# A two-layer transformer on one core: the order of results in the gated unit's groups

## The chip, the cores and the metric

One Trainium2 chip, one core of it. The metric is device time of one execution in microseconds. The kernel before took 1144.48 us, the median of 3 runs (1144.44 to 1144.59). Differences of a few tenths of a per cent matter here.

## The reference

Four sequences of 512 tokens with 256 features pass through two layers in fp32; each half layer normalises its input and adds its result to the residual. Layer 0 is causal attention with 16 heads and a mixture of 8 experts; layer 1 is attention with 16 query and 4 key heads, and a gated unit with weights of 4 bits. Only the last matters here:

```python
def _L1_ffn_ref(x, gate_W_packed, gate_scales, ...):
    ...
    Wg = dequant_nvfp4(gate_W_packed, gate_scales)
    ...
    gate = jnp.einsum('th,nh->tn', xt, Wg)
    up = jnp.einsum('th,nh->tn', xt, Wu)
    gelu = jnp.tanh(0.7978845608028654 * (gate + 0.044715 * gate ** 3)) * gate * 0.5 + gate * 0.5
    inter = gelu * up
    out = jnp.einsum('tn,hn->th', inter, Wd)
```

It has 2048 tokens, 256 features and 2048 inner units.

## The kernel before

**Engines and order.** TensorE (PE), VectorE (DVE), ScalarE (ACT) and GpSimd (POOL) run their instructions in the order in which the program writes them. The program is therefore a schedule written by hand: where a call stands decides where its instruction stands in its engine's queue. Only semaphores between engines make one wait for another.

**The last stage.** The gated unit runs over 4 blocks of 512 tokens (`j`) and, in each, 8 groups of 256 inner units (`jj`): 32 groups, `i = 8 j + jj`, in the loop at L1471. Groups 0 to 3 multiply plainly. Groups 4 to 31 (L1517 on, the branch that is changed) use a 2 x 2 scheme with 7 products in place of 8. Each `quarter` is one product: two matmuls, one for the gate weights and one for the up weights, which the trace shows as 4 matmul instructions. Besides the plain quarters of weights (`a11`, `a12`, `a22`) and tokens (`b11` and so on) the products read three sums of weights `s1`, `s2`, `s4`, the difference `s3` that takes the place of `a21`, and four sums of tokens `t`.

The products go into four PSUM tiles of 512 columns: `e` and `g`, two halves of `eg` (two buffers in turn), and `f` and `k` (one buffer each, called `gu_first` in the profile). The order on TensorE in one group is e, k, two down products, f, e, two down products, g, f, two down products, g, one down product. Between them stand:
- the copy f<-e (L1523), the copy p7<-k (L1529) and the copy g<-f (L1535) on ScalarE: the products after it add to what was copied;
- two additions on VectorE, `sb` upper = p7 + g (L1541) and `sb` lower = p7 + f (L1543). L1541 reads g before the last product adds to it, so that product waits for L1541.

**The results of the group before.** A group's gate and up values lie in `eg` (first half of the tokens) and `sb` (second half). Two generators make the activation of the *preceding* group, `eg_gelu` and `sb_gelu`, in four steps each: Square on ScalarE (L1405); a product on VectorE (L1407); Tanh on ScalarE (L1409); two products on VectorE, `th` and `it` (L1411, L1412). `done(i - 1)` then has GpSimd make three differences of the result `it` (L1314 with 512 columns, L1315 and L1316 with 256).

**Down products.** `down(n)` issues n matmuls of the second matrix product (L1336), which lags by two to three groups. Seven products take two groups. Their results go through ScalarE copies (L1348, L1356), VectorE additions (L1350, L1352, L1354, L1358, L1360) and, every second group, four GpSimd additions (L1362 to L1365). The two PSUM tiles `yx` and `yy` are used again by the next round: its first product needs L1360 of the round before to have read `yx`.

**Beside them.** `both()`, called twice in a group, advances the preparation of the next block: in group `jj` = 2 statistics (L1439, L1440), in 4 the normalising (four L1448), in 5 two transposes (L209) with DMAs issued by SP, in 7 the four token sums `t[0]`, `t[2]`, `t[1]`, `t[3]` (L1196 to L1199). `weight_sums(m)` makes s1, s3, s2, s4 of group `m` of every block (L1183, L1184, L1187, L1188), four additions on VectorE; for `jj` = 0 to 3 they are made in groups 4 to 7 and first read in groups 8 to 11.

Of the kernel before, what the change touches and what calls it, by code (L numbers as in the profile page):

```python
# [32 lines left out]
def tile_transformer(  # L33
# [18 lines left out]
    nc = tc.nc  # L52
# [411 lines left out]
    with ExitStack() as l0:  # L464
# [407 lines left out]
        done = blanked = 0  # L872
# [78 lines left out]
    def quarter(ps, terms, start=True):  # L951

        for i, (lhs, rhs) in enumerate(terms):
            for w in range(2):
                nc.tensor.matmul(  # L955
                    ps[:, w], lhsT=lhs(w), rhs=rhs, start=start and not i and not w,
                    stop=i == len(terms) - 1 and w == 1, skip_group_check=not start,
                )

    def unit(half, jj, par):  # L960
        return lambda w: wgu[:, w, half, jj, par * P : (par + 1) * P]

    def tokens(xT, half, n):
        return xT[:, half, n * 256 : (n + 1) * 256]

    def plainly(ps, xT, jj, par, n):
        quarter(ps, [(unit(half, jj, par), tokens(xT, half, n)) for half in range(2)])

    with ExitStack() as l1:
# [204 lines left out]
        def weight_sums(jj):  # L1174

            tt = nc.vector.tensor_tensor
            a11, a12, a21, a22 = (
                wgu[:, :, half, jj, par * P : (par + 1) * P] for par in range(2) for half in range(2)
            )
            s1, s2, s4 = (sums[jj - 4][:, :, i] for i in range(3))  # L1180

            def first():
                tt(s1, a21, a22, ALU.add)  # L1183
                tt(a21, a11, a21, ALU.subtract)  # L1184

            def second():
                tt(s2, s1, a11, ALU.subtract)  # L1187
                tt(s4, a12, s2, ALU.subtract)  # L1188

            return first, second  # L1190
# [89 lines left out]
    with ExitStack() as f1:  # L1280
# [16 lines left out]
        def down_unit(k, jj, m):  # L1297
            return wd[:, jj, k, m * P : (m + 1) * P]

        def down_weight_sums(jjs):  # L1300

            pool_tt = nc.gpsimd.tensor_tensor
            a11, a12, a21, a22 = (down_unit(k, jjs, m) for m in range(2) for k in range(2))
            s1, s2, s4 = (down_sums[:, jjs, i] for i in range(3))
            pool_tt(s1, a21, a22, ALU.add)
            pool_tt(a21, a11, a21, ALU.subtract)
            pool_tt(s2, s1, a11, ALU.subtract)
            pool_tt(s4, a12, s2, ALU.subtract)

        def unit_sums(i):  # L1310

            it = its[i]
            pool_tt = nc.gpsimd.tensor_tensor
            pool_tt(it[:, 4:6], it[:, 1:4:2], it[:, 0:2], ALU.subtract)  # L1314
            pool_tt(it[:, 6], it[:, 3], it[:, 4], ALU.subtract)  # L1315
            pool_tt(it[:, 1], it[:, 2], it[:, 6], ALU.subtract)  # L1316
# [55 lines left out]
        def down(n):  # L1372
            nonlocal next_down
            for _ in range(n):
                if next_down is not None and i >= 2 * next_down + 3:
                    next_down = next(downs, None)
# [49 lines left out]
        def done(i):  # L1426

            if i < NBLK * NJ - 2:
                unit_sums(i)
# [37 lines left out]
        f, k = firsts  # L1467
# [3 lines left out]
        for i in range(NBLK * NJ):  # L1471
            j, jj = divmod(i, NJ)
            if i == 3:
                nc.scalar.copy(last_a21, down_unit(0, slice(6, 8), 1))
            if i < 4:
                down_weight_sums(slice(2 * i, 2 * i + 2))
            if jj == 2 and j + 1 < NBLK:
                coming = next_inputs(j + 1)
            its[i] = d5.tile([P, 7, 256], F32, tag="it", name=f"it{i}")
            xT = xTs_f[j]  # L1480
            b11, b12, b21, b22 = (tokens(xT, half, n) for half in range(2) for n in range(2))
            if i < 2:
                egs.append(ps_eg.tile([P, 2, 2, 256], F32, tag="eg", name=f"eg{i}"))
            eg = egs[i % 2]
            e, g = eg[:, 0], eg[:, 1]
            sb = d2.tile([P, 2, 512], F32, tag="sb", name=f"sb{i}")
            eg_gelu, sb_gelu = before

            def both():
                if coming is not None:  # L1490
                    next(coming, None)

            if i < 4:
                eg_gelu.step()
                if not i:
                    nc.vector.tensor_copy(sb[:, :, :256], f)
                    nc.vector.tensor_copy(sb[:, :, 256:], k)
                plainly(e, xT, jj, 0, 0)
                sb_gelu.step()
                eg_gelu.step()  # L1500
                plainly(g, xT, jj, 0, 1)
                sb_gelu.step()
                eg_gelu.step()
                eg_gelu.step()
                sb_gelu.step()
                down(4)
                if i:
                    plainly(f, xT, jj, 1, 0)
                    nc.vector.tensor_copy(sb[:, :, :256], f)
                    sb_gelu.step()  # L1510
                    done(i - 1)
                    both()
                    down(3)
                    plainly(k, xT, jj, 1, 1)
                    nc.vector.tensor_copy(sb[:, :, 256:], k)
                    both()
            else:  # L1517
                t = [ts_f[j][:, n] for n in range(4)]
                s1, s2, s4 = (lambda w, n=n: sums[jj - 4][:, w, n] for n in range(3))
                a11, a12, s3, a22 = (unit(half, jj, par) for par in range(2) for half in range(2))  # L1520
                p7 = d2.tile([P, 2, 256], F32, tag="p7", name=f"p7_{i}")
                quarter(e, [(a11, b11)])
                nc.scalar.copy(f, e)  # L1523
                eg_gelu.step()
                eg_gelu.step()
                quarter(k, [(s3, t[2])])
                down(2)
                quarter(f, [(s2, t[1])], start=False)
                nc.scalar.copy(p7, k)  # L1529
                sb_gelu.step()  # L1530
                sb_gelu.step()
                eg_gelu.step()
                eg_gelu.step()
                quarter(e, [(a12, b21)], start=False)
                nc.scalar.copy(g, f)  # L1535
                sb_gelu.step()
                down(2)
                quarter(g, [(s1, t[0])], start=False)
                sb_gelu.step()
                done(i - 1)  # L1540
                tt(sb[:, :, 256:], p7, g, ALU.add)  # L1541
                quarter(f, [(a22, t[3])], start=False)
                tt(sb[:, :, :256], p7, f, ALU.add)  # L1543
                down(2)
                both()
                quarter(g, [(s4, b22)], start=False)
                down(1)
                both()
                if 4 <= i < 8:
                    for half in weight_sums(i - 4):  # L1550
                        half()
            before = (
                Gelu(f"{i}_0", eg[:, :, 0], eg[:, :, 1], its[i][:, 0:2]),
                Gelu(f"{i}_1", sb[:, 0], sb[:, 1], its[i][:, 2:4].rearrange("p n q -> p (n q)")),
            )
        eg_gelu, sb_gelu = before
# [76 lines left out]
```

## Time and profile before

| what | value |
|---|---|
| median of the runs | 1144.48 us |
| the profiled execution, its time and its span | 1144.61 us, 1142.9 us |
| granted TensorE clock | 1.00 throughout |
| 858 to 897 us (groups 4 to 7): TensorE, VectorE, GpSimd busy | 36.35, 35.55, 18.19 of 39 |
| 897 to 936 us (groups 8 to 11) | 37.90, 30.06, 16.87 of 39 |
| 936 to 1128 us (groups 12 to 31) | 187.62, 138.44, 83.96 of 192 |

A timeline row has the start and the busy time in microseconds, the engine, the line, the operation, the tile written and the tiles read, and the number of instructions that it merges; in brackets the idle time ahead of it and what ended it. Successive instructions of one engine overlap a little, so a row can start before the one ahead of it has ended. PEld is the weight load of a matmul, which can run beside the matmul before it.

### The profile page before, as it was taken

To read this page: it belongs to the slowest core of one execution; us is meant where nothing else is said; L and a number is where in the kernel's file an instruction comes from. 1 tells how busy PE (TensorE), PEld (TensorE's weight loads), DVE (VectorE), ACT (ScalarE), POOL (GpSimd) and SP (SyncE) were. 2 spreads that over 40 slices of the span, in tenths; PEclk is the share of its full clock that TensorE was granted. 3 is DMA by queue.
4 is the path that set the end of the run, shared out by engine and by line. 5 is a ranking of instruction groups with operands and counts; after the bars stand their busy time and mean duration, and the time that the engine had idled before them with its cause. 6 is when DMAs were issued, how large, how long until landed. Compare 5 with 4: busy or idle time off the path is not lost.

```text
span 1142.9 us, 19523 instructions
## 1 busy us (share of the span) xinstructions
PE 1113.0 (97%) x7474; PEld 716.1 (63%) x7474; DVE 844.6 (74%) x1856; ACT 509.8 (45%) x1190; POOL 247.1 (22%) x319
## 2 busy tenths in 40 slices
PE   9999999999999999999999999999999999999998
PEld 5666555555555445555555556656787788888885
DVE  6676989999988962867772695577479877778665
ACT  1445545565555543444444353344324444444442
POOL 8322221211112000000000000000064544353433
PEclk9999999999999999999999999999999999999999
DMA  4450110000000400000000001242001002002000
GB/s 133 113 130 2 21 20 1 2 1 2 1 2 1 156 29 1 1 1 1 1 1 0 1 1 38 65 111 65 20 1 45 30 19 74 1 19 74 18 3 19
DMA packets 30510, 34.92 MB, mean 31 GB/s; under 512 B 4280, under 2 KB 21432, under 8 KB 30416
## 3 DMA queue, kind: packets, MB, share of 16 engines
q1 hardware_dynamic: 29600, 32.49, 10.4%
q10 hardware_dynamic: 816, 1.18, 0.4%
q8 instruction: 59, 0.97, 0.3%
q14 instruction: 35, 0.29, 0.1%
HBM read 23.17 MB, written 6.29 MB: 26 GB/s over the span
## 4 chain that ended last, share of the span: by engine, by line
PE 69%; DVE 22%; ACT 3%; issue 2%; POOL 1%; SPq 1%; DMA 1%; DVEq 0%; POOLq 0%; ACTq 0%
PE qk_ps L1029 10%; PE lg_ps L249 9%; PE o L1120 8%; PE eo L249 7%; PE eg L955 7%; PE gu_first L955 5%; PE s L731 3%; PE yx L1336 3%; DVE mx L702 3%; PE s L683 3%; PE av L767 2%; PE yy L1336 2%; DVE it L1412 2%; DVE th L1411 2%; PE qk_ps L554 2%
## 5 line engine op out<-in xcount | busy, mean ns | idle before, releaser
L1029 PE MATMUL qk_ps<-xT,wqkv 128*128 128x512 f32 x320 | 148.7, 599 | 3.5 <-ACT v L1015 1.7
L249 PE MATMUL lg_ps<-rw,xT 128*128 128x512 f32 x256 | 122.5, 601 | 1.4 <-ACT xT L996 0.3
L249 PE MATMUL eo<-ew,xT 128*128 128x512 f32 x256 | 121.5, 600 | 0.8 <-ACT lg L312 0.5
L1120 PE MATMUL o<-wpj,oT 128*128 128x256 f32 x512 | 119.1, 382 | 0.0
L750 POOL TENSOR_SCALAR_AFFINE_SELECT pt<-pt 128x256 f32<-128x256 f32 (+2 forms) x88 | 62.4, 716 | 246.6 <-ACT pt L740 246.5
L1120 PEld LDWEIGHTS o<-wpj,oT 128*128 128x128 f32 x512 | 96.0, 190 | 27.0 <-issue 13.5
L1029 PEld LDWEIGHTS qk_ps<-xT,wqkv 128*128 128x128 f32 x320 | 59.1, 190 | 73.2 <-issue 58.4
L702 DVE TENSOR_REDUCE mx<-s 128x1 f32<-128x384 f32 (+3 forms) x176 | 100.4, 632 | 0.0
L740 ACT ACTIVATE pt<-s 128x512 f32<-128x512 f32 (+1 forms) x176 | 84.1, 564 | 35.8 <-PE s L731 35.8
L182 POOL TENSOR_TENSOR ln_rs<-rs_v,minus_half 128x4 f32<-128x4 f32 x12 | 13.6, 1131 | 366.2 <-DVE rs_v L181 366.2
L338 ACT ACTIVATE part<-eo,c 128x256 f32<-128x256 f32 x128 | 53.6, 472 | 84.6 <-PE eo L249 74.7
L1523 ACT COPY gu_first<-eg 128x512 f32<-128x512 f32 x28 | 16.0, 570 | 134.2 <-PE eg L955 129.9
L249 PEld LDWEIGHTS lg_ps<-rw,xT 128*128 128x128 f32 x256 | 46.1, 190 | 46.1 <-issue 37.3
L249 PEld LDWEIGHTS eo<-ew,xT 128*128 128x128 f32 x256 | 46.1, 190 | 45.7 <-issue 38.3
L312 ACT COPY lg<-lg_ps 128x512 f32<-128x512 f32 x64 | 37.7, 588 | 73.5 <-PE lg_ps L249 73.5
L1314 POOL TENSOR_TENSOR it<-it 128x512 f32<-128x512 f32 x30 | 38.2, 1273 | 146.6 <-PE gu_first L955 66.9
L1033 ACT COPY qT<-qk_ps 128x512 f32<-128x512 f32 x64 | 37.5, 586 | 64.7 <-PE qk_ps L1029 64.7
L1336 PE MATMUL yx<-it,wd 128*128 128x256 f32 x240 | 66.2, 379 | 0.0
L683 PE MATMUL s<-qk 32*128 32x128 f32 (+3 forms) x512 | 56.8, 465 | 0.2
L438 DVE SCALAR_TENSOR_TENSOR junk<-lg,w 128x256 bf16<-128x256 f32 x128 | 55.1, 430 | 0.0
L365 DVE TENSOR_TENSOR part<-part 128x512 f32<-128x512 f32 x32 | 22.5, 704 | 43.9 <-ACT part L338 43.9
L731 PE MATMUL s<-qk 32*128 32x128 f32 x1280 | 54.4, 287 | 0.5
(306 smaller groups left out, 2231.9 us busy)
## 6 DMA issues: line engine op xcount, KB each, us to landing
qk<-stage SPq DMA_DIRECT2D x56, 64.0 KB, 2.4
wqkv<-in_w_qkv SPq DMA_DIRECT2D x8, 320.0 KB, 7.1
rw<-in_router_w SPq DMA_DIRECT2D x8, 256.0 KB, 4.7
ew<-in_expert_w SPq DMA_DIRECT2D x8, 256.0 KB, 5.3
wpj<-in_w_proj SPq DMA_DIRECT2D x1, 2048.0 KB, 11.0
dq_sgu<-in_gate_up_s SPq DMA_DIRECT2D x64, 32.0 KB, 2.1
xres<-in_x SPq DMA_DIRECT2D x3, 512.0 KB, 4.8
xT_rows<-xT SPq DMA_DIRECT2D x12, 128.0 KB, 2.4
```

Of the source, the lines that this page charges most:

```text
L249: nc.tensor.matmul(ps, lhsT=xT[:, hc, (g % 4) * P : (g % 4 + 1) * P], rhs=w[:, hc, 2 * pair : 2 * pair + 2, :].rearrange("p e o -> p (e o) ...
L338: nc.scalar.mul(part[:, e % 4], ps[:, i], c[:, e : e + 1])
L438: stt(junk, d[:, e], 0.0, w1, ALU.is_gt, ALU.mult, accum_out=c1[:, e : e + 1])
L683: nc.tensor.matmul(tiles[h][:, b * nk : (b + 1) * nk].rearrange("p (c k) -> p c k", k=P), lhsT=queries(j, g)[r, s], rhs=qk[r, g, : j + 1, ...
L702: nc.vector.tensor_reduce(maxes[n % 2][:, h, gs[0] : gs[0] + nb], ps[:, : nb * nk].rearrange("p (b k) -> p b k", b=nb), AX.X, ALU.max,)
L731: nc.tensor.matmul(tiles[h][:, at : at + P], lhsT=qk[r, g, c, s, :], rhs=queries(j, g)[r, s], start=True, stop=True,)
L740: nc.scalar.activation(pt[:, i, : nb * nk], tiles[2 * pair + i][:, : nb * nk], AF.Exp, scale=0.25)
L750: nc.gpsimd.affine_select(out=last, in_=last, compare_op=ALU.is_ge, fill=0.0, base=0, pattern=pattern, channel_multiplier=-1,)
L955: nc.tensor.matmul(ps[:, w], lhsT=lhs(w), rhs=rhs, start=start and not i and not w, stop=i == len(terms) - 1 and w == 1, skip_group_check= ...
L1029: nc.tensor.matmul(ps, lhsT=wqkv[:, hc, kv, h, :], rhs=xT[:, hc, :], start=hc == 0, stop=hc == 1,)
L1120: nc.tensor.matmul(ys[t // 2][:, t % 2], lhsT=state["o"][:, h, t * P : (t + 1) * P], rhs=wpj[:, HPK * kv + h, :], start=kv == 0 and h == 0 ...
L1336: nc.tensor.matmul(ps, lhsT=lhs(jj), rhs=its[8 * j + jj][:, plane], start=start and not n, stop=n == 1, skip_group_check=not start,)
```

## The change

In groups 4 to 31 some steps trade places on ScalarE, VectorE and GpSimd; TensorE's and SP's order stays.
- The first step of `eg_gelu` (Square) stands ahead of the group's first copy, its second step between the product and the copy; the first two steps of `sb_gelu` follow the copy.
- The copy p7<-k moves from ahead of these steps to behind the third step of `sb_gelu` (Tanh).
- The fourth step of `sb_gelu` (`th` and `it`) and `done(i - 1)` move behind both additions into `sb`.
- The weight sums of `jj` = 0 to 3 are made in groups 7 to 10 instead of 4 to 7, each in the group just before the one that reads it first.

```diff
+                eg_gelu.step()
                 quarter(e, [(a11, b11)])
+                eg_gelu.step()
                 nc.scalar.copy(f, e)
-                eg_gelu.step()
-                eg_gelu.step()
+                sb_gelu.step()
+                sb_gelu.step()
                 quarter(k, [(s3, t[2])])
                 down(2)
                 quarter(f, [(s2, t[1])], start=False)
-                nc.scalar.copy(p7, k)
-                sb_gelu.step()
-                sb_gelu.step()
                 eg_gelu.step()
                 eg_gelu.step()
                 quarter(e, [(a12, b21)], start=False)
                 nc.scalar.copy(g, f)
                 sb_gelu.step()
+                nc.scalar.copy(p7, k)
                 down(2)
                 quarter(g, [(s1, t[0])], start=False)
-                sb_gelu.step()
-                done(i - 1)
                 tt(sb[:, :, 256:], p7, g, ALU.add)
                 quarter(f, [(a22, t[3])], start=False)
                 tt(sb[:, :, :256], p7, f, ALU.add)
+                sb_gelu.step()
+                done(i - 1)
                 down(2)
                 both()
                 quarter(g, [(s4, b22)], start=False)
                 down(1)
                 both()
-                if 4 <= i < 8:
-                    for half in weight_sums(i - 4):
+                if 7 <= i < 11:
+                    for half in weight_sums(i - 7):
                         half()
```

## Prediction

> **What bounds the kernel now.** I read the page first, then the list of waits of the last stage (858 to 1128 us), then the timeline of one group of it, engine by engine.
>
> ```profile
> PE 1113.0 (97%) x7474; PEld 716.1 (63%) x7474; DVE 844.6 (74%) x1856; ACT 509.8 (45%) x1190; POOL 247.1 (22%) x319
> ```
>
> TensorE sets the end. The change touches groups 4 to 31 of the last stage only, so what counts is TensorE's idle time there, and which engine ends it. The waits of that stretch (engine and line that waited, releaser, sum in us, times, longest):
>
> ```profile
> PEld eg L955 <- DVE sb L1541: 12.7, 16, 0.8
> PEld eg L955 <- ACT eg L1535: 10.0, 28, 1.9
> ```
>
> Two waits, both of a matmul that writes g: it waits for the copy g<-f (L1535), and for the addition that reads g (L1541). PEld counts from an idle weight load, so these sums are not TensorE's loss. The loss comes from the starts of the first copy of each group:
>
> ```profile
> L1523 ACT COPY gu_first<-eg x28: 570/570/570, 858.3 to 1119.2; 128x512 f32<-128x512 f32 x28
> ```
>
> 27 group periods take 260.9 us. A group is 42 matmul instructions, and they start 0.216 apart (rows 965.15 to 968.61 below: 16 in 3.46), so an unbroken group is 9.08 us and 27 are 245.3: 15.6 lost, with the last group's own waits 16.4. One group of it, number 15 (TensorE; then ScalarE, VectorE, GpSimd):
>
> ```profile
> 965.15 1.03 PE L955 MATMUL eg<-xT,wgu 128*128 128x256 f32 x4
> 966.01 1.03 PE L955 MATMUL gu_first<-t,wgu 128*128 128x256 f32 x4
> ...
> 968.61 1.03 PE L955 MATMUL eg<-xT,wgu 128*128 128x256 f32 x4
> 969.47 1.03 PE L1336 MATMUL yy<-it,down_sums 128*128 128x256 f32 x4
> 970.39 1.13 PE L955 MATMUL eg<-t,late_sums 128*128 128x256 f32 x4
> 971.36 1.03 PE L955 MATMUL gu_first<-t,wgu 128*128 128x256 f32 x4
> 972.22 1.03 PE L1336 MATMUL yx<-it,wd 128*128 128x256 f32 x4
> 973.69 1.13 PE L955 MATMUL eg<-xT,late_sums 128*128 128x256 f32 x4 [0.44 <-DVE sb L1541]
> ```
> ```profile
> 969.74 0.60 ACT L1535 COPY eg<-gu_first 128x512 f32<-128x512 f32 x1
> ```
> ```profile
> 972.34 0.69 DVE L1412 SCALAR_TENSOR_TENSOR it<-th,sb 128x512 f32<-128x512 f32 x1
> 972.95 0.68 DVE L1541 TENSOR_TENSOR sb<-p,eg 128x512 f32<-128x512 f32 x1
> ...
> 974.14 0.41 DVE L1352 TENSOR_TENSOR x<-x,yx 128x256 f32<-128x256 f32 x1
> 974.48 0.42 DVE L1196 TENSOR_TENSOR t<-xT 128x256 f32<-128x256 f32 x1
> 974.81 0.95 DVE L1197 TENSOR_TENSOR t<-xT 128x256 f32<-128x256 f32 x1
> 975.68 0.94 DVE L1198 TENSOR_TENSOR t<-xT,t 128x256 f32<-128x256 f32 x1
> ```
> ```profile
> 973.18 1.27 POOL L1314 TENSOR_TENSOR it<-it 128x512 f32<-128x512 f32 x1 [4.20 <-DVE it L1412]
> 974.53 0.95 POOL L1315 TENSOR_TENSOR it<-it 128x256 f32<-128x256 f32 x1
> 975.56 0.79 POOL L1316 TENSOR_TENSOR it<-it 128x256 f32<-128x256 f32 x1
> ```
>
> Read: the g product at 973.69 starts 0.60 late, because L1541 stood in VectorE's queue behind a down result and th and it of sb (L1350, L1411, L1412; 971.29 to 972.95). The one at 970.39 is 0.06 late, and a matmul run that had to wait is 0.10 longer (1.13 for 1.03). The last two fences carry the forecast: beside L1315 and L1316 an addition of two SBUF tensors takes 0.95 instead of 0.42, and the two engines take turns.
>
> **The change, part by part.** Times below are from a group's first product (row 965.15); its stages start 0.865 apart, the next group at 9.08. A result is read 1.07 after its product starts (the copy that follows 965.15 starts at 966.22).
>
> *Square first, copies of p later (ScalarE).* Its input is complete at 7.79 + 1.07 of the group before, 0.22 ahead of this group, where ScalarE is idle (4.31 us in this group): free. Then copy f 1.07 to 1.64, Square of sb to 2.2, a down copy from 2.8 to 3.2 (odd groups), tanh to 3.8, copy g to 4.3. Needed at 5.19: the first wait goes, 0.9 to spare. tanh of sb and copy p end by 5.4; L1541 wants p at 6.26. No DMA moves past another on any queue: the DMAs of the pieces come from SP, in the same order.
>
> *sb additions ahead of the down results (VectorE).* The g result comes at 5.19 + 1.07; VectorE has by then only Square's products, the e results (to 5.2) and one down addition (5.4 to 5.8), so the addition runs 6.26 to 6.94. Needed at 7.79: the second wait goes, 0.85 to spare.
>
> *What goes:* all 16.4 except 0.2 at group 4, whose product k waits for the copy L1515 of group 3, which stays. **-16.2.** This includes 1.8 at group 5, where the moved weight sums stood.
>
> *What is late next.* th and it of sb now follow both additions: the second starts at 7.12 (6.06 + 1.07), th at 7.72, it at 8.44. Before, the it of sb came ahead of them (972.34, that is 7.19). All that follows in VectorE's queue moves with it, and so does L1314, which starts 0.84 after it (972.34 to 973.18): 9.28 to 10.55. In a plain group nobody waits for that: L1315's plane is read by the down product at 4.3 of the next group but ends at 2.3, and the down addition that frees its bank for the product at 1.73 ends at 0.7. But three things stand behind it.
>
> (a) *Token sums of a new block* (end of groups 7, 15, 23), read by the second product of the next group, at 9.08 + 0.87 = 9.95. Before, they started 0.61 ahead of the next group and t2 (L1197) ended at 975.76, just ahead of need. Now t0 comes at 9.38, inside L1314. No row shows such an addition meet L1314 in its middle, so I bound it. Nothing held: t2 ends at 10.13 and TensorE loses 0.35. Held: t0 ends 0.28 after L1314 (975.48 to 975.76 is that distance for L1315), 10.83; L1315 is next and ends 0.58 later (974.90 to 975.48), 11.41; t2 at 11.69; TensorE 0.06 later, 11.75. That is 1.8 and 0.1 for the unhidden weight load: 1.9. I take the held one, since the rows above show exactly this alternation. Groups 16 and 24: 3.8.
>
> (b) *Weight sums* now at the end of groups 7 to 10, read in the next group: s3 (L1184), the second of four, by its second product. VectorE makes four in 1.6 us unhindered (879.80 to 881.43), in 2.6 to 3.3 beside GpSimd (rows of L1183 to L1188: 0.42 each, or up to 0.65 to 0.95). Group 8: they follow all four token sums: t1 12.5, t3 13.0, s1 13.4, s3 13.8, so 4.0 lost (free 2.0). Groups 9 and 10: s1 and s3 stand where t0 and t2 did: 1.9 each (free 0.8 and 0.5). Group 11: four statistics (0.60 each) and a down addition come first; s1 at 11.9, s3 at 13.3: 3.5 (free 3.0).
>
> (c) *Normalising for the next block* (end of groups 4, 12, 20): two L1448 stand ahead of the down addition L1360, whose bank the next group's first down product (10.82) needs. Before:
>
> ```profile
> 945.41 1.73 DVE L1448 TENSOR_SCALAR xn<-xres,ln_mv,ln_rs 128x256 f32<-128x256 f32 x2
> 947.07 0.41 DVE L1360 TENSOR_TENSOR x<-x,yx 128x256 f32<-128x256 f32 x1
> ```
>
> L1360 ended 1.5 into group 13, 0.3 ahead of need. Now the first L1448 waits for L1314 (10.55 + 0.15), the second for L1315 (to 11.5), L1360 ends at 11.84: 1.1 and 0.1, 1.2 each (free: none). Three: 3.6. Statistics alone (group 18) make the same product 0.2 late.
>
> Sum of the new: 3.8 + 4.0 + 3.8 + 3.5 + 3.6 + 0.2 = **+18.9**; with nothing held 0.7 + 2.0 + 1.3 + 3.0 + 0 + 0.2 = 7.2. In each of these groups the late VectorE work (Square's product at 2.8 at worst; copy g ends 1.9 after it) still meets 5.19, so a delay isn't paid twice. The tail after group 31 keeps its order and follows its last product. Net +2.7 on the profiled 1144.61 (span 1142.9 and 1.7 around it; the median of the runs is 1144.48): **1147.3**.
>
> The Trainium skill (SBUF — State Buffer, "SBUF: two separate sides") has the port pair of VectorE and GpSimd as an exclusive lock, held for the whole instruction, for a VectorE operation with two SBUF inputs too. By it an addition would start its whole 0.42 only after GpSimd's end, where the row shows 0.28: 1.4 more over these places, 1148.7.
>
> **The rivals.** *The port doesn't hold (faster).* If an addition reached during L1314 runs at its 0.42, the new waits are 7.2 and the time 1135.6. For it: the additions into sb read PSUM beside L1314 and take 0.68 as ever; and what counts is who asks first, with t0 asking 0.10 after L1314 started. Against: L1448 took up to 0.93 beside L1315. It decides from a hold under 40% of mine (7.2 + 0.4 x 11.7 = 11.9, that is 1140.3; the break-even is at 77%). *VectorE wins the race* against L1314 at groups 8, 10, 16, 24 and for L1448: t2 ends near 11.2, 0.5 less each, and 0.35 less at each L1448: 1144.3, no change. *One steady wait stays (slower still).* p is copied behind both tanh; if Square's product of sb is held behind GpSimd's additions to x by 1.8 us more than I allow, L1541 is late again in every second group, at 0.3 or more: 4 more, 1151. *The change doesn't do what it says*: the g waits stay as they are and the new ones come on top, 1163; I see no row for it.
>
> **How the numbers follow.** Forecast 0.60: the steady waits go and the new ones come nearly in full, 1144 to 1150. It gives slower 0.42, same 0.17, faster 0.01. Port free 0.20: faster 0.17, same 0.03. Race won 0.10: same 0.08, faster 0.02. Steady wait stays, or no effect, 0.10: slower. Together faster 0.20, same 0.28, slower 0.52; 0.2% is 2.3 us, about what a measurement of this kernel tells from no change. The range, 1138 to 1151, leaves out most of the free port and the far end.
>
> **What would show it.** Right: plain groups at 9.08 us with no wait of a g product; the second product of groups 8, 9, 10, 11, 16 and 24 waiting for VectorE (4.0, 1.9, 1.9, 3.5, 1.9, 1.9); a down product of groups 5, 13 and 21 waiting for L1360 by 1.2; t0 and t2 near 0.9 to 1.4 us. Wrong: t0 and t2 at 0.42, group 16 starting its second product on time, or groups 25 to 31 longer than 9.2.

## The result, and the profile after

The changed kernel took 1151.51 us, the median of 6 runs (1149.79 to 1152.85), the kernel before 1144.53 (6 runs, 1144.44 to 1144.62): ratio 1.0060, 95% interval 1.0049 to 1.0071. It is slower, as forecast, but by 7.0 us and not by 2.7, and outside the range. The profiled execution is the fastest of the six, 1149.79 (span 1148.1).

The busy times on the page are nearly as before (TensorE again 97%). The changed kernel's list of waits from 858 to 1140 us (sum, times, longest), and the starts of each group's first copy:

```profile
PE gu_first L955 <- DVE wgu L1184: 10.5, 4, 3.9
...
PEld eg L955 <- ACT eg L1534: 8.8, 28, 0.8
...
PE gu_first L955 <- DVE t L1197: 3.5, 2, 1.7
```
```profile
L1525 ACT COPY gu_first<-eg x28: 570/570/570, 858.2 to 1125.1; 128x512 f32<-128x512 f32 x28
```

The wait for the addition into sb, 12.7 us before, is gone from the list. The wait for the copy g<-f (L1535 before, L1534 now) is still there, in all 28 groups. New are the waits of the second product for the weight sums (L1184) and the token sums (L1197). The 27 group periods now take 266.9 us instead of 260.9.

Group 15 again, TensorE and then ScalarE (it starts at 972.60 here):

```profile
976.05 1.03 PE L955 MATMUL eg<-xT,wgu 128*128 128x256 f32 x4
976.91 1.03 PE L1336 MATMUL yy<-it,down_sums 128*128 128x256 f32 x4
977.79 1.13 PE L955 MATMUL eg<-t,late_sums 128*128 128x256 f32 x4
...
980.49 1.03 PE L955 MATMUL eg<-xT,late_sums 128*128 128x256 f32 x4
```
```profile
977.17 0.57 ACT L1534 COPY eg<-gu_first 128x512 f32<-128x512 f32 x1 [0.88 <-PE eg L955]
```

The last g product is on time now (1.03 long, no gap). The first one still shows 1.13: its weight load is not hidden. ScalarE was idle for 0.88 ahead of the copy g<-f and began as the second e product ended (976.05 + 1.07). So the copy waits for that e product too, not only for f.

The end of group 15, VectorE and then GpSimd:

```profile
981.15 0.69 DVE L1412 SCALAR_TENSOR_TENSOR it<-th,sb 128x512 f32<-128x512 f32 x1
...
982.09 1.44 DVE L1196 TENSOR_TENSOR t<-xT 128x256 f32<-128x256 f32 x1
983.45 0.94 DVE L1197 TENSOR_TENSOR t<-xT 128x256 f32<-128x256 f32 x1
```
```profile
981.98 1.26 POOL L1314 TENSOR_TENSOR it<-it 128x512 f32<-128x512 f32 x1 [3.04 <-DVE it L1412]
```

t0 was reached 0.1 after L1314 had started, and ended 0.28 after L1314's end; L1315 followed at 983.33, then t2.

Last, TensorE around group 11, and a window there (length, busy time of TensorE, weight loads, VectorE, ScalarE and GpSimd, then the granted clock, here 0.53, the DMA share and GB/s):

```profile
930.10 1.03 PE L955 MATMUL eg<-xT,wgu 128*128 128x256 f32 x4
934.37 1.38 PE L955 MATMUL gu_first<-t,wgu 128*128 128x256 f32 x4 [3.25 <-DVE wgu L1184]
935.54 1.91 PE L1336 MATMUL yx<-it,wd 128*128 128x256 f32 x4
937.25 1.67 PE L955 MATMUL gu_first<-t,first_sums 128*128 128x256 f32 x4
```
```profile
935.00:938.60 3.60, 3.60 (x11) 2.86 (x10) 2.38 (x5) 0.90 (x2) 1.63 (x2) 0.53 0.31 125
```

After an idle time of 3.25 us four matmuls take 1.7 us instead of 0.865: the clock is at a half from 935.1 to 938.5, 3.4 us, and costs 1.7. Before, the clock of this stage was 1.00 throughout.

The six executions fit stretches of this price: without any the changed kernel would take about 1148.1; the two at a granted clock of 0.998 took 1149.8 and 1150.2, the two at 0.996 and 0.997 took 1151.5, the two at 0.995 took 1152.8, which is about one, two and three stretches (one lowers the mean clock of the span by 0.0015). Only the fastest has a trace, so for the other five the count is an estimate from time and clock.

The profiled execution, term by term (group periods beyond a plain group's 9.18, from the starts of the first copies):

| term | forecast | measured |
|---|---|---|
| steady waits removed | -16.2 | -13.4 (28 x 0.1 stays) |
| (a) token sums, groups 16, 24 | 3.8 | 3.9 |
| (b) weight sums, groups 8, 9, 10, 11 | 4.0, 1.9, 1.9, 3.5 | 4.1, 1.9, 2.0, 3.5 |
| (c) normalising, groups 5, 13, 21; statistics, 19 | 3.6; 0.2 | 1.7; 0 |
| half clock | none | 1.7 |
| sum | +2.7 | +5.4 (1149.79 - 1144.61 = 5.2) |

### The profile page after: what moved, and what is told of

Its sections match the earlier page's. It is cut to its first block, busy times and chain, and to the rows that moved or that the text cites. A ratio compares the mean times of both kernels' runs of the same rounds, so it can differ in the third digit from the quotient of the medians.

```text
span 1148.1 us, 19550 instructions
## 1 busy us (share of the span) xinstructions
PE 1111.5 (97%) x7474; PEld 719.2 (63%) x7474; DVE 856.8 (75%) x1856; ACT 513.8 (45%) x1190; POOL 255.6 (22%) x319
## 3 DMA queue, kind: packets, MB, share of 16 engines
q1 hardware_dynamic: 29600, 32.49, 10.9%
## 4 chain that ended last, share of the span: by engine, by line
PE 74%; DVE 19%; issue 2%; ACT 2%; POOL 1%; DMA 1%; SPq 0%; POOLq 0%; ACTq 0%; DVEq 0%
PE qk_ps L1029 10%; PE lg_ps L249 9%; PE eg L955 8%; PE o L1120 8%; PE gu_first L955 7%; PE eo L249 7%; PE yx L1336 4%; PE s L731 3%; DVE mx L702 3%; PE s L683 3%; PE yy L1336 3%; PE av L767 2%; PE qk_ps L554 2%; PE v_ps L1011 1%; PE s L1042 1%
## 5 line engine op out<-in xcount | busy, mean ns | idle before, releaser
L750 POOL TENSOR_SCALAR_AFFINE_SELECT pt<-pt 128x256 f32<-128x256 f32 (+2 forms) x88 | 63.6, 730 | 245.3 <-ACT pt L740 245.2
L1314 POOL TENSOR_TENSOR it<-it 128x512 f32<-128x512 f32 x30 | 38.1, 1271 | 147.8 <-PE yx L1336 87.1
L955 PE MATMUL gu_first<-t,wgu 128*128 128x256 f32 x192 | 50.0, 383 | 14.0 <-DVE wgu L1184 10.5
L1405 ACT ACTIVATE sq<-eg 128x512 f32<-128x512 f32 x32 | 19.1, 597 | 87.0 <-PE eg L955 75.0
```

Of the source, the lines that this page charges most:

```text
L750: nc.gpsimd.affine_select(out=last, in_=last, compare_op=ALU.is_ge, fill=0.0, base=0, pattern=pattern, channel_multiplier=-1,)
L955: nc.tensor.matmul(ps[:, w], lhsT=lhs(w), rhs=rhs, start=start and not i and not w, stop=i == len(terms) - 1 and w == 1, skip_group_check= ...
```

## The experiments

**e1: weight sums back in groups 4 to 7.**

```diff
-                if 7 <= i < 11:
-                    for half in weight_sums(i - 7):
+                if 4 <= i < 8:
+                    for half in weight_sums(i - 4):
```

> The changed kernel with the weight sums made in groups 4 to 7 again; the rest of the change stays. Theory (the moved sums are most of the loss): the waits of groups 9, 10 and 11 (1.8, 1.9, 3.4 us) go, that of group 8 falls from 4.0 to the token sums' 1.9, and with them the half-clock stretch that followed the 3.4 us wait; groups 5 to 7 give 3 to 5 back. 1142 to 1145 us, granted clock 1.000. Rival (the reordering of results in the group is the loss, the sums matter little): 1148 us or more.

Measured: 1146.04 us (11 runs, 1144.52 to 1147.74), ratio 1.0008 (1.0000 to 1.0017), 1.0 above my range. Groups 9, 10 and 11 take 9.18 us each, the second product of group 8 waits 1.9. But group 5, where sums and normalising meet, is longer than I thought (TensorE of e1):

```profile
871.01 1.03 PE L1336 MATMUL yy<-it,down_sums 128*128 128x256 f32 x4
875.46 2.08 PE L955 MATMUL eg<-t_first,late_sums 128*128 128x256 f32 x4 [3.42 <-ACT eg L1534]
```

The wait there is 3.4 us, and half clock follows for 6.8. So the place of the sums is most of the loss (5.5 us of 7.0), and the rival, that the reordering is the loss, falls; that the old place is harmless under the new order falls too.

**e2: the kernel before, with the weight sums moved alone** (the edit of e1 the other way round, in the kernel before).

> The kernel before with nothing but the weight sums moved to groups 7 to 10. Theory: with the old order VectorE reaches the end of a group about 0.9 us sooner, so the new waits are smaller than in the changed kernel: 2 at group 8, 0.2 to 1 at 9, at most 0.3 at 10, 2 to 2.7 at 11, against 2 saved in groups 5 to 7: 1146.5 to 1148.5 us, no wait over 3 us and clock 1.000. Rival (the sums alone bring the whole loss): 1151 us or more.

Measured: 1149.36 us (5 runs, 1148.04 to 1149.72), ratio 1.0031 (1.0019 to 1.0043). In the profiled execution (1148.04) the waits are 2.0, 1.3, 0 and 2.7 at groups 8 to 11, near what I expected (group 9 was to wait 1 at most), and the clock is 1.00. The median is 0.9 above my range; that three of the five executions had one half-clock stretch more is likely from the step of 1.3 to 1.7 us and from their granted clock, 0.998 or 0.999 where the other two have 1.000, but only one execution has a trace, so it isn't shown. The sums alone cost 4.6 us, less than the 5.5 under the new order, where VectorE comes to them 0.9 us later; the rival, that they are the whole loss, falls.

**e3: one down product moved behind the second e product.**

```diff
                 quarter(k, [(s3, t[2])])
-                down(2)
+                down(1)
...
                 nc.scalar.copy(p7, k)
-                down(2)
+                down(3)
```

> The changed kernel with one of the first two down products moved behind the group's second e product. The copy g<-f waits for that e product (it starts as soon as it ends, in every group), and the g product after it then starts with an unhidden weight load, 0.105 us in each of 28 groups. Here the e product ends 0.43 us earlier and one more down product stands behind it. Theory: plain groups fall from 9.18 to 9.08 us, 2.9 us in all: 1148.5 us beside 1151.5. Rival (the load is unhidden for another reason): plain groups stay at 9.18 and the time at 1151.5.

Measured: 1149.99 us (5 runs, 1148.33 to 1150.94), ratio 1.0039 (1.0027 to 1.0051). Plain groups take 9.07 us instead of 9.18. Group 15 of e3, TensorE and ScalarE:

```profile
977.74 1.03 PE L955 MATMUL eg<-xT,wgu 128*128 128x256 f32 x4
978.61 0.59 PE L1336 MATMUL yx<-it,wd 128*128 128x256 f32 x2
979.04 1.03 PE L1336 MATMUL yy<-it,down_sums 128*128 128x256 f32 x4
979.90 1.03 PE L955 MATMUL eg<-t,late_sums 128*128 128x256 f32 x4
```
```profile
978.86 0.57 ACT L1534 COPY eg<-gu_first 128x512 f32<-128x512 f32 x1 [1.44 <-PE eg L955]
```

The copy still starts as the e product ends, but three down matmuls stand behind that product now, and the g product is 1.03 long. The theory holds for the groups; the medians differ by 1.5 only. Half-clock stretches are the likely reason: the profile of e3 has three (one in an early stage) to the other's one, and its five executions a granted clock of 0.993 to 0.996, those of the changed kernel 0.995 to 0.998.

**e4: GpSimd's differences held back until the token sums are made** (groups 7, 15, 23).

```diff
-                done(i - 1)
+                held = jj == 7 and j + 1 < NBLK
+                if not held:
+                    done(i - 1)
                 down(2)
                 both()
+                if held:
+                    after_sums = d2.tile([P, 1], F32, tag="after_sums", name=f"after_sums{j}")
+                    nc.gpsimd.tensor_copy(after_sums, ts_f[j + 1][:, 3, :1])
+                    done(i - 1)
```

> The changed kernel with GpSimd's three differences at the end of groups 7, 15 and 23 held back until the token sums of the new block are made (a GpSimd copy of one column of the last sum stands ahead of them); same results. Theory (the token sums are slow because they take turns with GpSimd's differences): t0, t2, t1 and t3 take 0.42 each, the waits of groups 16 and 24 fall from 1.9 to 0.3, that of group 8 from 4.0 to about 2.3: 4.5 to 5 us less. Rival (they are late because of their place in the queue alone, or slow by themselves): these waits stay at 1.5 or more.

Measured: 1147.49 us (12 runs, 1144.18 to 1149.91), ratio 1.0013 (1.0004 to 1.0022), 4.0 under the changed kernel. VectorE at the end of group 15:

```profile
983.02 0.42 DVE L1196 TENSOR_TENSOR t<-xT 128x256 f32<-128x256 f32 x1
983.36 0.42 DVE L1197 TENSOR_TENSOR t<-xT 128x256 f32<-128x256 f32 x1
```
GpSimd starts only at 984.63. At the same place in VectorE's queue, without GpSimd beside it, each sum takes 0.42, and groups 16 and 24 take 9.60 us, 0.4 over a plain group: both ends of the forecast's bound are measured, and the rival, that the place in the queue alone makes them late, falls. Group 8 still waits 3.0 where I expected 2.3: there the held-back L1314 (897.33) meets s3 (L1184, 897.36), which takes 1.51.

**e5: weight sums behind groups 1, 2 and 3.**

```diff
                     nc.vector.tensor_copy(sb[:, :, 256:], k)
                     both()
+                    for m in ((0,), (1,), (2, 3))[i - 1]:
+                        for half in weight_sums(m):
+                            half()
...
-                if 7 <= i < 11:
-                    for half in weight_sums(i - 7):
-                        half()
```

> The changed kernel with the weight sums made behind groups 1, 2 and 3 (one, one and two sets), where VectorE stands idle for about a third of the time and no gated group has begun; the order inside the gated groups stays as changed. Theory (new waits of 9.5 us come from the place of the sums, and each wait of 3 us or more can bring a half-clock stretch of 3.4 us, 1.7 us of time): no wait at groups 9 to 11, 1.9 at group 8, 0.6 at group 5, clock 1.000 in this stage; 1138.5 us and 0 to 2.5 for the sums in their new place: 1138.5 to 1141, so 0.3 to 0.5% under the kernel before. Rival (the reordering itself costs): 1145 or more.

Measured: 1144.83 us (11 runs, 1144.19 to 1144.90), ratio 0.9999 (0.9990 to 1.0008). From group 4 on all is as expected: 256.4 us between the first copies instead of 266.9. That is also 4.5 under the kernel before, so the rival, that the reordering itself costs, falls. But the first copy of group 4 comes 5.5 us later, and TensorE of e5 shows why:

```profile
853.23 1.89 PE L955 MATMUL gu_first<-x_first,wgu 128*128 128x256 f32 x8
857.82 1.37 PE L1336 MATMUL yx<-it,wd 128*128 128x256 f32 x4 [2.71 <-ACT y_p L1348]
```

A down product of group 3 waits 2.7 us for the copy L1348, which stands in ScalarE's queue behind the activation that VectorE delays, and half clock follows. My price for the new place, 0 to 2.5, was too low.

**e6: waits of eight lengths, to measure the clock.** The kernel of b1 below, with

```diff
+        fillers = {9: 1, 11: 2, 14: 3, 17: 4, 19: 5, 22: 6, 25: 8, 28: 12}
...
+                for _ in range(fillers.get(i, 0)):
+                    t2 = ts_f[j][:, 2]
+                    nc.vector.tensor_copy(t2, t2)
```

> Measures the clock by itself. The kernel of b1_all with 1, 2, 3, 4, 5, 6, 8 and 12 copies of a token sum onto itself on VectorE behind groups 9, 11, 14, 17, 19, 22, 25 and 28, which the next group's second product has to wait for: waits of about 1, 1.8, 2.3, 2.8, 3.2, 3.6, 4.5 and 6.2 us, same results. Theory (a wait of about 3 us or more is followed by a 3.4 us stretch of half clock): stretches behind the last four or five waits, none behind the waits under 2.7. Rival (the stretches come at any time, as in one execution of the first stage, and have nothing to do with the wait): stretches are not tied to these groups.

Measured: 1174.18 us (4 runs), ratio 1.0256 (1.0241 to 1.0272). The waits became 0.8, 1.7, 2.4, 2.7, 3.1, 4.7, 4.1 and 7.0. Half clock follows the six from 2.4 on, one or two more than I expected, and not the two shorter ones, so the stretches are tied to the waits and the rival falls: 3.4 us behind the first three, 6.8 behind the next two, 10.2 behind the last. Three windows, with the same columns, the step with the 2.4 in it, the half-clock one behind it, and the step with the 2.7:

```profile
965.99:969.40 3.41, 1.16 (x6) 0.70 (x5) 3.34 (x6) 1.20 (x3) 3.25 (x5) 1.00 0.50 154
969.40:972.81 3.41, 3.41 (x10) 2.66 (x9) 1.86 (x3) 0.55 (x1) 2.48 (x3) 0.50 0.00 0
996.70:1000.10 3.40, 1.19 (x6) 0.71 (x4) 3.31 (x5) 1.64 (x3) 2.71 (x3) 1.00 0.00 0
```

The stretches start at 969.4, 1000.1, 1024.0, 1054.8, 1088.9 and 1123.0: 9, 7, 9, 10 and 10 times 3.41 apart. So the clock is set in steps of 3.41 us, and a step in which TensorE was idle for 2.2 us brings half clock for the next. That explains the changed kernel: counted back from 935.1, a step ends at 897.6 and cuts the idle time of group 8 (895.6 to 899.4) into 2.0 and 1.9, and no stretch followed there; that of group 11 lies with 2.7 in one step. In this stage the threshold is between 2.0 and 2.2 in all traces. Where the steps fall differs from one execution to the next, and with it the number of stretches.

Idle time of this kind is not the only thing that halves the clock. The traces of e3, e4 and b2 each have one stretch in the first layer (from 26.7, 188.4 and 188.1 us), behind a step in which TensorE was idle for 0.2 us or less; most of its matmuls there have 32 rows or columns in place of 128, but no run shows that this is the reason. The kernel before, too, took 1146.2 to 1146.3 us at a clock of 0.998 in 7 of its 23 executions beside e1 to e4, and none of these has a trace.

**b1: all three repairs.** e3 and e5 together, and `both()` ahead of the last step of `sb_gelu`:

```diff
                 tt(sb[:, :, :256], p7, f, ALU.add)
+                both()
                 sb_gelu.step()
                 done(i - 1)
                 down(2)
-                both()
```

> The changed kernel with three edits: weight sums behind groups 1 to 3, the first call of the next block's preparation ahead of th and it of sb instead of behind them, and one of the first two down products moved behind the second e product. Theory: the token sums (t2 at 8.5 us into the group) and the normalising no longer meet GpSimd's differences, so the waits of groups 8, 16, 24 (1.9 each) and 5, 13, 21 (0.6 each) go too, and plain groups take 9.08 us: 16.2 under the kernel before, 0 to 2.5 given back in groups 1 to 3: 1128 to 1131 us. Rival (th and it of sb, now later still in those groups, bring a new wait of the next group): 1133 or more.

Measured: 1134.04 us (4 runs, 1133.21 to 1135.65), ratio 0.9907 (0.9893 to 0.9920). No wait is left from group 5 on, all groups take 9.06 or 9.07. What is above the forecast is in groups 2, 3 and 4: waits of 0.6, 2.9 and 1.7, the place of e5's sums again. So the time is where the rival put it, but not for the rival's reason.

**b2: weight sums spread.** b1 with one set behind group 1, and in place of the others

```diff
                 both()
+                if i in (6, 8, 9):
+                    for half in weight_sums({6: 1, 8: 2, 9: 3}[i]):
+                        half()
                 sb_gelu.step()
```

> b1_all with the weight sums in other places: one set behind group 1, the others in groups 6, 8 and 9 between the two additions into sb and th of sb, where the token sums cost nothing in b1_all. In b1_all the sets behind groups 2 and 3 made TensorE wait 0.7 us, 2.9 us (a down product that waits for the copy L1348) and 1.7 us (one that waits for L1354). Theory: these waits go and no new one comes, every group from 4 on takes 9.07 us: 1128 to 1130 us, clock 1.000. Rival (four additions there push th and it of sb so far that the next group's copy of g is late): 0.5 to 1 us at groups 7, 9 and 10, 1130 to 1132.

Measured: 1129.52 us (4 runs, 1129.46 to 1129.67), ratio 0.9869 (0.9852 to 0.9885): 14.9 us under the kernel before. Groups 7 and 9 take 9.48 and 9.47, with a wait for a down addition (L1358, shown below), group 4 takes 9.25, the rest at most 9.07. The 27 periods between its first copies (859.4 to 1105.1) take 245.7 us, where the prediction reckoned 245.3 for an unbroken stage.

## Why the prediction was wrong

The direction and most terms held; the size failed at three steps, and one of them is a term that the sum lacked.

- **Where the median failed most: no term for the clock.** The sum counted each wait at its own length. A wait that leaves TensorE idle for 2.2 us or more of one step also halves its clock for one or more steps of 3.41 us, 1.7 us of time each while it has work. The profiled execution has one, 1.7; by time and clock the two at the median had two, 3.4, and the slowest (1152.85, clock 0.995) three. e6 shows the mechanism with waits made for it. The trace of before could not show it: its clock is 1.00 through the stage, and TensorE's longest gap there is 1.5 us. The Trainium skill (TensorE: Matmul & The Clock Gate, "Part 1: The HAM clock gate") has a free-running window of about 3.4 us and half clock after at least one idle window. The steps of 3.41 us agree. Read as a whole window without work, the condition does not: 2.2 of 3.41 were enough.
- **"The first wait goes, 0.9 to spare."** It doesn't go, 28 x 0.1 = 2.8 stays, the largest term that failed in the profiled execution. I let the copy g<-f start when f was complete and ScalarE free. It waits for the second e product as well, which was to be seen in the trace of before (the same line idle until an e product, 10.9 us in 12 groups). In group 15 it ran from 4.57 to 5.14, and though the product was due at 5.19 its weight load had to wait. e and g are halves of one tile, and a copy into one half was ordered behind the product into the other; that this is the reason is argued, since no run had them in two tiles. That the wait for e makes the 0.1 is shown by e3. It is not the wait of the rival *One steady wait stays*, which came near in time (1151): that one was L1541's, for a late p, and it went.
- **(c), normalising: 1.7, not 3.6.** I let the first down product wait for L1360, the reader of `yx`. It did not wait: in group 13 it started at 955.39, before L1360 at 956.01 (the changed kernel's TensorE and VectorE, then a line of b2's waits):

```profile
955.39 1.03 PE L1336 MATMUL yx<-it,wd 128*128 128x256 f32 x4
959.42 1.13 PE L955 MATMUL eg<-t,late_sums 128*128 128x256 f32 x4 [0.42 <-ACT eg L1534]
```
```profile
956.01 0.41 DVE L1360 TENSOR_TENSOR x<-x,yx 128x256 f32<-128x256 f32 x1
...
957.55 0.67 DVE L1407 SCALAR_TENSOR_TENSOR sq<-sq,eg 128x512 f32<-128x512 f32 x1
```
```profile
PEld yx L1336 <- DVE x_first L1358: 1.1, 2, 0.5
```

So what I wrote of `yx` and `yy`, that a round's first product needs L1360 of the round before, is wrong: in b2 that product waits for L1358, the reader of `yy`, which stands ahead of the normalising. That the two tiles trade their banks from round to round fits this but is argued. What was late in group 13 was the next thing I had named there, Square's product (957.55, 3.9 into the group, where I had 2.8 at worst) and with it the copy g: 0.6 in groups 5, 13 and 21. In this size the error helped the forecast, by 1.9, and that is luck.

- **Right: (a) and (b).** The alternation of VectorE and GpSimd was taken from L1315 and L1316 and carried to L1314, which no row showed: 1.97 measured at groups 16 and 24 for 1.9, and (b) within 0.1 at each of its four groups. e4 measures the other bound, 0.4 for 0.35. The rival of the free port falls with it, and so does that of VectorE winning the race: t0 started 0.1 after L1314 and ended 0.28 after its end, as the forecast took it, not a whole 0.42 after.
- **Right: the second steady wait.** The addition into sb no longer delays any group, and th and it of sb behind it cost nothing in plain groups.

With the three steps put right the forecast's own working gives 1147.3 + 2.8 - 2.1 = 1148.0 without the clock, and 1149.7 with one stretch; 1149.79 was measured. With two it is 1151.4, beside the median of 1151.51.

## What to carry to other kernels

Work that is moved behind a critical operation must be followed to its own reader: here two waits went, 0.5 us a group together, and the new place of the token sums and of 16 weight sums gave it all back in six groups, with the clock and the normalising on top. A wait that sits in one place for 3 us can cost more than six of 0.5, since the clock can fall after it; so late work is better spread over groups with room, one set each, than made just ahead of its reader. For each copy into a shared tile, read which product it truly waited for in the trace, not the one that the data needs.

## What the runs showed of the hardware

- The clock of TensorE is set in steps of 3.41 us: in the last stage a step at full clock with 2.2 us idle or more was followed by one at half clock, steps with 2.0 us idle or less were not. An idle time of 3.85 us cut in two by a step's end passed without a stretch.
- A half-clock step that was itself idle for 1.0 us or more was followed by another (e6), one with 0.3 or less by full clock; with 0.6 it went once each way (e1, e4). So a wait that reaches into the half-clock step lengthens the stretch to 6.8 or 10.2 us.
- An addition of two SBUF tensors on VectorE (128x256, 0.42 us alone) that arrives during a GpSimd operation of 1.26 us ended 0.28 after that operation's end and showed 1.44; the two engines then took turns. A VectorE addition that reads PSUM kept its time beside GpSimd (0.68 for L1541 at 972.95 in the kernel before, with L1314 from 973.18).
